# Two layers of cross-attention: layer 0's softmax weights transposed on VectorE in 32x32 blocks instead of on TensorE

## The chip, the cores and the metric

The kernel runs on one core of a Trainium2 chip. The metric is device time in microseconds: the median of several executions. A profiled execution has a time of its own, and a span, from its first instruction to its last, that is a little shorter.

The engines are named as the profile names them: PE is TensorE (matmuls), PEld its weight loads, DVE is VectorE, ACT is ScalarE, POOL is GpSimd, SP is the queue that issues most DMAs. L450 is line 450 of the kernel.

## The reference

All data are fp32. Eight batches have 100 query rows of width 1024 and a context of 1444 rows of width 512. Layer 0 is cross-attention with an output projection and a residual. Layer 1 takes its softmax over the query axis (axis 1, the 100 rows), adds its input and normalises.

```python
# x (8,100,1024), ctx_512 (8,1444,512)
# layer 0
Q = x @ Wq + bq; K = ctx @ Wk + bk; V = ctx @ Wv + bv
weights = softmax(Q @ K^T / sqrt(1024), axis=-1)        # (8,100,1444)
x = x + (weights @ V) @ Wo + bo
# layer 1
q = x @ Wq + bq; k = ctx @ Wk + bk; v = ctx @ Wv + bv
w = softmax(q @ k^T / sqrt(1024), axis=1)               # over the 100 rows
y = w @ v + x
out = (y - mean) * rsqrt(var + 1e-6) * gamma + beta
```

## The kernel before, in words

The kernel multiplies weight matrices with each other first (Wq with Wk, Wv with Wo), so that the long context never has to be projected: queries are brought into the 512-wide space of the context (`gT`), scores are taken against the raw context, and the weighted sum of raw context rows is projected afterwards. The big products are done with seven half-size products in place of eight.

**Layer 0's attention** is what the change touches. For each batch b there are three pieces of work.

- `scores0` (matmul L480, called "s" below): scores of the 100 queries against the context, 4 parts of the 512-wide axis times 11 pieces of the 1444 columns, so 44 matmuls. The context comes transposed (`cT`, four loads of 128x1444, `load_features`). The results fill four PSUM banks of the six that the pool `psum` has. VectorE moves them to the tile `p` (100x1444) with scale and bias (L492), takes the negative maximum (L494), ScalarE takes the exponential and the sum (L496), VectorE the reciprocal (L498) and the scaling (L499).
- `transposed` (L511, L512): `p` has queries on its rows, and the weighted sum needs context rows there. TensorE transposes 12 blocks of 100x120 (the last group 100x124), in three groups of four; each group goes into one PSUM bank, and ScalarE copies it to the tile `w`.
- `weighted_rows` (matmul L450, called "A"): 12 chunks of 120 context rows (the last one 124) times 4 parts of 128 columns, so 48 matmuls that add up in one PSUM bank of the pool `psum2`, which has two. VectorE copies the result to `A0T` (L463). The rows come through `load_rows` (L429, L433), four tiles of three chunks. Each load names 128 rows of every chunk, of which 120 are used.

**Order.** TensorE's order is the order of the program text; the other engines' orders are made by a scheduler from dependencies. The loop at L755 does iteration b: A of batch b, alternating one matmul for one with s of batch b+2, and the three transpose groups of batch b+1 put in after steps 28, 34 and 40. The scores of batches 0 and 1 and all of batch 0's transposes stand before the loop. In iterations 6 and 7 no scores are left, so A runs alone. After iteration 7 comes `project0`, then layer 1's queries and its own attention loop, which uses `weighted_rows` for its last two batches.

**Buffers.** Context tiles of both kinds share one pool of ten, and an iteration uses eight. SP issues a load when the tile of ten loads earlier is free. The `p` tiles come from a pool of three; the same three later hold three rows for layer 1 (`row_on_all`, L772, issued by POOL).

An fp32 matmul shows in the profile as two records, a transpose as one.

Of the kernel before, what the change touches and what calls it, by code (L numbers as in the profile page):

```python
# [24 lines left out]
F32 = mybir.dt.float32  # L25
# [14 lines left out]
GM = 4  # L40
NP, PM = 11, 3
CUTS = [S * n // NP for n in range(NP + 1)]
G = 4
GT = G * T
G1 = 5
# [5 lines left out]
def two_layer_cross_attention(ctx: ExitStack, tc: tile.TileContext, a: dict, out: bass.AP):  # L51
# [11 lines left out]
    def bank(name):  # L63
        return psum.tile([P, 512], F32, tag="ps", name=name)
# [11 lines left out]
    def row(name):  # L76
        return work.tile([P, E], F32, tag="row", name=name, bufs=3)

    def probabilities(name):
        return work.tile([P, S], F32, tag="prob", name=name, bufs=3)  # L80


    ones = const.tile([P, P], F32, tag="ones", name="ones")
# [9 lines left out]
    def column(name, layout):  # L93
        t = const.tile([P, EC], F32, tag=name, name=name)
        nc.gpsimd.dma_start(out=t, in_=a[name].rearrange(layout, c=EC))
        return t
# [3 lines left out]
        for n in ("L0_xattn_bq", "L0_xattn_bk", "L0_xattn_bv", "L1_xattn_bq", "L1_xattn_bk")  # L100
    }
    out_bias = column("L0_xattn_bo", "(c p) -> p c")

# [307 lines left out]
    def load_columns(b):  # L413

        src = a["ctxT"][b].rearrange("(c p) m -> p c m", p=P)
        for q in range(NQ):
            t = unit(f"cT_{b}_{q}")[:, : LC * (QR + MX)].rearrange("p (c m) -> p c m", c=LC)
            nc.sync.dma_start(out=t, in_=src[:, :, q * QR : (q + 1) * QR + MX])
            yield t

    def load_rows(b):

        src = a["ctx_512"][b]
        for q in range(NQ):
            t = unit(f"c_{b}_{q}").rearrange("p (c l) -> p c l", c=CQ)
            n = CQ - (q == NQ - 1)

            rows = bass.AP(src.tensor, src.offset + q * QR * L, [[L, P], [MR * L, n], [1, L]])
            nc.sync.dma_start(out=t[:, :n, :], in_=rows)  # L429
            if n < CQ:  # L430
                m = (MC - 1) * MR
                for r0, r1 in ((0, 112), (112, MR + MX)):
                    nc.sync.dma_start(out=t[r0:r1, n, :], in_=src[m + r0 : m + r1, :])  # L433
            yield t
# [6 lines left out]

        return MR + (MX if c == MC - 1 else 0)

    def weighted_rows(w, c, dst, name):

        ps = bank2(name)
        for m in range(MC):
            r = held(m)
            for k in range(LC):
                nc.tensor.matmul(  # L450
                    ps[:, k * T : (k + 1) * T],
                    c[m // CQ][:r, m % CQ, k * P : (k + 1) * P],
                    w[:r, m, :],
                    start=(m == 0 and k == 0),
                    stop=(m == MC - 1),
                    skip_group_check=True,
                )
                if (m, k) == (MC - 1, LC - 1):
                    src = ps[:, :GT].rearrange("p (c t) -> p c t", t=T)
                    if name.startswith("A1"):  # L460
                        nc.scalar.copy(dst, src)
                    else:
                        nc.vector.tensor_copy(dst, src)  # L463
                yield


    def scores0(s, cT):

        b = s["b"]
        p = probabilities(f"p_{b}")[:T]
        q0 = gT[0][b // G]
        t0 = b % G * T
        banks = [bank(f"s0_{b}_{n}") for n in range(0, NP, PM)]
        for k in range(LC):
            for n in range(NP):
                o = CUTS[n // PM * PM]
                nc.tensor.matmul(  # L480
                    banks[n // PM][:T, CUTS[n] - o : CUTS[n + 1] - o],
                    q0[:, k, t0 : t0 + T],
                    cT[k][:, CUTS[n] : CUTS[n + 1]],
                    start=(k == 0 and n % PM == 0),
                    stop=(k == LC - 1),
                    skip_group_check=True,
                )
                if (k, n) != (LC - 1, NP - 1):
                    yield
        for n, ps in zip(range(0, NP, PM), banks):  # L490
            o, e = CUTS[n], CUTS[min(n + PM, NP)]
            nc.vector.tensor_scalar(p[:, o:e], ps[:T, : e - o], SCALE, c0[:, b : b + 1], ALU.mult, ALU.add)  # L492
        negmax = small.tile([T, 1], F32, tag="negmax", name=f"negmax_{b}")
        nc.vector.tensor_reduce(negmax, p, AX.X, ALU.max, negate=True)  # L494
        total = small.tile([T, 1], F32, tag="total", name=f"total_{b}")
        nc.scalar.activation(p, p, AF.Exp, bias=negmax, accum_out=total)  # L496
        rtotal = small.tile([T, 1], F32, tag="rtotal", name=f"rtotal_{b}")
        nc.vector.reciprocal(rtotal, total)  # L498
        nc.vector.tensor_scalar(p, p, rtotal, None, ALU.mult)  # L499
        s["p"] = p  # L500
        yield

    def transposed(s):

        b, p = s["b"], s["p"]
        w = s["w"] = work.tile([P, MC, T], F32, tag="wT", name=f"w0_{b}", bufs=3)
        for m0 in range(0, MC, GM):
            ps = bank(f"pT_{b}_{m0}")
            r = shown(m0)
            for m in range(m0, m0 + GM):  # L510
                nc.tensor.transpose(ps[:r, (m - m0) * T : (m - m0 + 1) * T], p[:, m * MR : m * MR + r], ident[:T, :T])  # L511
            nc.scalar.copy(w[:r, m0 : m0 + GM, :], ps[:r, :GT].rearrange("p (c t) -> p c t", t=T))  # L512
            yield

    def add_to_queries(blocks, t0, width, banks):
        n = len(blocks) // len(banks)
# [42 lines left out]
    def scores1(s, cT, c1):  # L559

        b = s["b"]
        q1 = gT[1][b // G]
        t0 = b % G * T
        w = s["w"] = work.tile([P, MC, T], F32, tag="wT", name=f"w1_{b}", bufs=3)
        negmax = small.tile([P, MC], F32, tag="negmax1", name=f"negmax1_{b}")
        total = small.tile([P, MC], F32, tag="total1", name=f"total1_{b}")
        rtotal = small.tile([P, MC], F32, tag="rtotal1", name=f"rtotal1_{b}")  # L570
        for m0 in range(0, MC, GM):
            ps = bank(f"s1_{b}_{m0}")
            r = shown(m0)
            for m in range(m0, m0 + GM):
                o = m % CQ * MR
                for k in range(LC):
                    nc.tensor.matmul(  # L577
                        ps[:r, (m - m0) * T : (m - m0 + 1) * T],
                        cT[m // CQ][:, k, o : o + r],
                        q1[:, k, t0 : t0 + T],  # L580
                        start=(k == 0),
                        stop=(k == LC - 1),
                    )
                    if (m, k) != (m0 + GM - 1, LC - 1):
                        yield
            grp = slice(m0, m0 + GM)
            nc.vector.scalar_tensor_tensor(  # L587
                w[:r, grp, :],
                ps[:r, :GT].rearrange("p (c t) -> p c t", t=T),
                SCALE,  # L590
                c1[:r, t0 : t0 + T].unsqueeze(1).to_broadcast([r, GM, T]),
                ALU.mult,
                ALU.add,
            )
            nc.vector.tensor_reduce(negmax[:r, grp], w[:r, grp, :], AX.X, ALU.max, negate=True)  # L595
            for m in range(m0, m0 + GM):
                nc.scalar.activation(  # L597
                    w[:r, m, :], w[:r, m, :], AF.Exp, bias=negmax[:r, m : m + 1], accum_out=total[:r, m : m + 1]
                )
            nc.vector.reciprocal(rtotal[:r, grp], total[:r, grp])  # L600
            nc.vector.tensor_tensor(
                w[:r, grp, :], w[:r, grp, :], rtotal[:r, grp].unsqueeze(2).to_broadcast([r, GM, T]), ALU.mult
            )
            yield
# [146 lines left out]

    for b in range(2):
        run(scores0(batches[b], *loaded(load_features(b))))
    run(transposed(batches[0]))
    for b in range(B):  # L755
        nxt = b + 2 < B
        c, *cT = loaded(load_rows(b), *([load_features(b + 2)] if nxt else []))
        A = weighted_rows(batches[b]["w"], c, A0[b // G][:, :, b % G * T : (b % G + 1) * T], f"A0_{b}")
        s0 = scores0(batches[b + 2], *cT) if nxt else iter(())
        wT = transposed(batches[b + 1]) if b + 1 < B else iter(())  # L760
        for n in range(MC * LC):
            next(A)
            next(s0, None)
            if n in (28, 34, 40):
                next(wT, None)
        if b == 1:
            AS = value_sums(wvo)
    project0(AS, A0)

    def row_on_all(name):  # L770
        t = probabilities(name)[:, :E]
        nc.gpsimd.dma_start(out=t, in_=a[name].partition_broadcast(P))  # L772
        return t

    gT[1] = queries(1, wqk1, u1)
    c1 = [key_bias1(0)]
    bv1 = row_on_all("L1_xattn_bv")
    gamma = row_on_all("L1_xattn_gamma")
    beta = row_on_all("L1_xattn_beta")
    wv1 = weights.tile([P, LC, E], F32, tag="w", name="wv1")  # L780
    nc.gpsimd.dma_start(out=wv1, in_=a["L1_xattn_Wv"].rearrange("(c p) e -> p c e", p=P))
    for b in range(2):
# [7 lines left out]
    for b in range(B):  # L790
# [8 lines left out]
        if nxt:  # L799
            A = attend1(batches[b], c)  # L800
            s1 = scores1(batches[b + 2], *cT, c1[(b + 2) // G])
        else:
            A = weighted_rows(batches[b]["w"], c, A1[b][1], f"A1_{b}")
            s1 = iter(())
        for n in range(MC * LC):
            next(s1, None)
# [42 lines left out]
```

## Time and profile before

| | |
|---|---|
| median of 3 executions | 663.86 us (663.24 to 664.1) |
| the profiled execution | 663.64 us |
| its span | 661.7 us |
| TensorE busy | 650.8 us |
| VectorE busy | 359.8 us |
| ScalarE busy | 101.1 us |
| mean granted TensorE clock | 0.997 |
| layer 0: first score matmul to last A | 193.6 to 361.5 us |
| one iteration of the loop with scores | 20.7 us |
| its VectorE and ScalarE work | 5.65 and 3.07 us |

A busy time of TensorE counts instructions that overlap in its pipeline: what a matmul costs is read from the distance of two starts, not from the length that is listed for one. "Idle before" in a group's row is what its engine stood still ahead of it, and costs nothing where the engine isn't the one that sets the end.

### The profile page before, as it was taken

To read this page: it belongs to the slowest core of one execution; us is meant where nothing else is said; L and a number is where in the kernel's file an instruction comes from. 1 tells how busy PE (TensorE), PEld (TensorE's weight loads), DVE (VectorE), ACT (ScalarE), POOL (GpSimd) and SP (SyncE) were. 2 spreads that over 40 slices of the span, in tenths; PEclk is the share of its full clock that TensorE was granted. 3 is DMA by queue.
4 is the path that set the end of the run, shared out by engine and by line. 5 is a ranking of instruction groups with operands and counts; after the bars stand their busy time and mean duration, and the time that the engine had idled before them with its cause. 6 is when DMAs were issued, how large, how long until landed. Compare 5 with 4: busy or idle time off the path is not lost.

```text
span 661.7 us, 10338 instructions
## 1 busy us (share of the span) xinstructions
PE 650.8 (98%) x4360; PEld 552.8 (84%) x4360; DVE 359.8 (54%) x651; ACT 101.1 (15%) x295; POOL 22.8 (3%) x31
## 2 busy tenths in 40 slices
PE   9999999999999999999999999999999999999995
PEld 8885445568899999999999555579999999989992
DVE  5979638996055133312331875268443443566994
ACT  1010100321101111101120000204232322210000
POOL 2000000000000000000000000000000000001431
PEclk9999999999999999999999999999999999999998
DMA  9937046000099788988999003028888999820221
GB/s 295 378 121 264 0 121 255 1 0 1 26 347 310 247 291 291 315 291 293 311 327 345 30 0 127 1 87 285 267 297 297 307 307 296 299 78 1 77 74 50
DMA packets 60234, 127.51 MB, mean 193 GB/s; under 512 B 3928, under 2 KB 22872, under 8 KB 60188
## 3 DMA queue, kind: packets, MB, share of 16 engines
q1 hardware_dynamic: 57742, 119.82, 52.9%
q0 software_dynamic: 2048, 6.56, 3.1%
q8 instruction: 34, 0.56, 0.4%
q10 hardware_dynamic: 398, 0.47, 0.2%
q14 instruction: 12, 0.10, 0.0%
HBM read 123.56 MB, written 3.28 MB: 192 GB/s over the span
## 4 chain that ended last, share of the span: by engine, by line
PE 91%; DVE 5%; DMA 1%; issue 1%; SPq 1%; POOL 0%; POOLq 0%; DVEq 0%
PE A L450 14%; PE s L480 12%; PE s L577 12%; PE A L633 10%; PE qk_x L116 5%; PE g_x L116 5%; PE qk_y L116 4%; PE o_x L116 4%; PE g_y L116 3%; PE vo_x L116 3%; PE o_y L116 3%; PE qk_w L116 2%; PE vo_y L116 2%; PE g_w L116 2%; PE g_z L116 2%; PE o_w L116 1%
## 5 line engine op out<-in xcount | busy, mean ns | idle before, releaser
L450 PE MATMUL A<-w,c 120*128 120x100 f32 x960 | 146.2, 268 | 0.0
L450 PEld LDWEIGHTS A<-w,c 120*128 120x128 f32 x960 | 129.2, 191 | 0.1
L577 PE MATMUL s<-g1T,cT 128*120 128x100 f32 (+1 forms) x768 | 123.2, 261 | 0.0
L480 PE MATMUL s<-cT,g0T 128*100 128x131 f32 (+1 forms) x704 | 122.8, 275 | 0.0
L633 PE MATMUL A<-c,w 120*100 120x128 f32 (+1 forms) x576 | 110.7, 273 | 0.0
L577 PEld LDWEIGHTS s<-g1T,cT 128*120 128x120 f32 (+1 forms) x768 | 105.1, 185 | 0.6 <-issue 0.3
L480 PEld LDWEIGHTS s<-cT,g0T 128*100 128x100 f32 x704 | 87.8, 167 | 0.0
L633 PEld LDWEIGHTS A<-c,w 120*100 120x100 f32 (+1 forms) x576 | 74.0, 168 | 0.0
L492 DVE TENSOR_SCALAR p<-s,c 100x394 f32<-100x394 f32 (+2 forms) x32 | 18.8, 593 | 90.0 <-PE s L480 89.8
L597 ACT ACTIVATE w<-w,negmax 120x100 f32<-120x100 f32 (+1 forms) x96 | 35.1, 366 | 75.3 <-DVE negmax L595 75.3
L587 DVE SCALAR_TENSOR_TENSOR w<-s,c 120x400 f32<-120x400 f32 (+1 forms) x24 | 13.8, 574 | 41.6 <-PE s L577 41.6
L116 PE MATMUL qk_x<-qk 128*128 128x256 f32 x128 | 29.2, 387 | 0.0
L116 PEld LDWEIGHTS qk_x<-qk 128*128 128x128 f32 x128 | 24.5, 195 | 4.2 <-ACT qk L234 0.4
L512 ACT COPY w<-pT 120x400 f32<-120x400 f32 (+1 forms) x24 | 11.6, 493 | 100.3 <-PE pT L511 100.3
L708 POOL TENSOR_TENSOR rstd<-rstd,mhalf 100x1 f32<-100x1 f32 x8 | 11.8, 1477 | 230.6 <-DVE rstd L707 230.6
L600 DVE RECIPROCAL rtotal<-total 120x4 f32<-120x4 f32 (+1 forms) x24 | 4.2, 177 | 28.2 <-ACT w L597 28.2
L496 ACT ACTIVATE p<-p,negmax 100x1444 f32<-100x1444 f32 x8 | 12.0, 1499 | 46.9 <-DVE negmax L494 46.9
L519 DVE TENSOR_TENSOR xT<-xT,o_x 128x400 f32<-128x400 f32 (+1 forms) x24 | 13.7, 601 | 8.3 <-PE o_x L116 7.9
L597 ACT ACTIVATION_READ_ACCUMULATOR w<-w,negmax 120x1 f32 (+1 forms) x96 | 17.9, 187 | 0.0
L258 DVE SCALAR_TENSOR_TENSOR qk_L_xattn_bk<-qk,L_xattn_bk,qk_L_xattn_bk 128x1024 f32<-128x1024 f32 x14 | 17.8, 1271 | 0.0
L614 DVE TENSOR_REDUCE part<-w 120x100 f32<-120x1100 f32 x8 | 17.2, 2150 | 0.0
L323 DVE SCALAR_TENSOR_TENSOR kb<-xT,wqbk,kb 128x400 f32<-128x400 f32 x28 | 16.9, 626 | 0.2
(198 smaller groups left out, 862.2 us busy)
## 6 DMA issues: line engine op xcount, KB each, us to landing
c<-in_ctx SPq DMA_DIRECT2D x48, 768.0 KB, 8.1
cT<-in_ctxT SPq DMA_DIRECT2D x32, 728.0 KB, 6.4
cT<-in_ctxT SPq DMA_DIRECT2D x32, 722.0 KB, 5.9
c<-in_ctx SPq DMA_DIRECT2D x16, 512.0 KB, 7.6
vo<-in_L_xattn_Wo SPq DMA_DIRECT2D x8, 512.0 KB, 7.2
qk<-in_L_xattn_WqT SPq DMA_DIRECT2D x8, 512.0 KB
qk<-in_L_xattn_WqT SPq DMA_DIRECT2D x15, 256.0 KB, 5.4
qk<-in_L_xattn_WkT SPq DMA_DIRECT2D x15, 256.0 KB, 6.3
```

Of the source, the lines that this page charges most:

```text
L116: nc.tensor.matmul(banks[n // per][:, n % per * width : (n % per + 1) * width], lhs[i][:, n * P : (n + 1) * P], rhs[i], start=(fresh and i ...
L258: nc.vector.scalar_tensor_tensor(acc, src, cols[v][:, h : h + 1], acc, ALU.mult, ALU.add)
L323: nc.vector.scalar_tensor_tensor(acc, src, wqbk[:, k : k + 1], acc, ALU.mult, ALU.add)
L450: nc.tensor.matmul(ps[:, k * T : (k + 1) * T], c[m // CQ][:r, m % CQ, k * P : (k + 1) * P], w[:r, m, :], start=(m == 0 and k == 0), stop=( ...
L480: nc.tensor.matmul(banks[n // PM][:T, CUTS[n] - o : CUTS[n + 1] - o], q0[:, k, t0 : t0 + T], cT[k][:, CUTS[n] : CUTS[n + 1]], start=(k == ...
L492: nc.vector.tensor_scalar(p[:, o:e], ps[:T, : e - o], SCALE, c0[:, b : b + 1], ALU.mult, ALU.add)
L519: nc.vector.tensor_tensor(to, to, ps[:, : n * width].rearrange("p (n t) -> p n t", n=n), ALU.add)
L577: nc.tensor.matmul(ps[:r, (m - m0) * T : (m - m0 + 1) * T], cT[m // CQ][:, k, o : o + r], q1[:, k, t0 : t0 + T], start=(k == 0), stop=(k = ...
L587: nc.vector.scalar_tensor_tensor(w[:r, grp, :], ps[:r, :GT].rearrange("p (c t) -> p c t", t=T), SCALE, c1[:r, t0 : t0 + T].unsqueeze(1).to ...
L597: nc.scalar.activation(w[:r, m, :], w[:r, m, :], AF.Exp, bias=negmax[:r, m : m + 1], accum_out=total[:r, m : m + 1])
L614: nc.vector.tensor_reduce(part[:MR], w[:MR, :last, :].rearrange("p c t -> p t c"), AX.X, ALU.add)
L633: nc.tensor.matmul(ps[:T, part], w[:r, m, :], c[m // CQ][:r, m % CQ, part], start=(m == 0 and k == 0), stop=(m == MC - 1), skip_group_chec ...
```

## The change

1. `p` lies in three constant tiles of 1472 columns. POOL clears rows 96 to 127 and the columns from 1444 on of each once, at the start.
2. ScalarE moves the scores from PSUM with scale and bias; VectorE takes a maximum of each of the four parts and then of the four. ScalarE also does the scaling by the reciprocal.
3. Chunks of layer 0 have 128 context rows: eleven of 128 and one of 36. Their loads (`load_full_rows`) bring each row once.
4. The weights of a batch are transposed by VectorE: for each of four column quarters (of the 100 queries, padded to 128) and each of four row quarters of a chunk, one instruction transposes the 32x32 blocks of all 12 chunks (11 for the two row quarters that the last chunk doesn't have). That is 16 instructions a batch. A block's columns beyond 100 spill into the next chunk's place and are overwritten by a later instruction of the four quarters, which run from the last to the first.
5. For batches 0 and 7, TensorE still transposes the first four chunks in one group, with one ScalarE copy (`first_transposed`), and VectorE the other eight. The group stands directly ahead of the batch's A.
6. In the iteration b=5, two score matmuls stand beside each A, so that the last batch's scores end half-way through it.

```diff
+QD = 32
+SC = -(-S // P)
+SW = (SC - 1) * P + 2 * QD
+PT = 4
...
+    prob = [const.tile([P, SW], F32, tag=f"prob{n}", name=f"prob{n}") for n in range(3)]
+    for t in prob:
+        nc.gpsimd.memset(t[T // QD * QD :, :], 0.0)
+        nc.gpsimd.memset(t[:, S:], 0.0)
...
+    def load_full_rows(b):
...
+            full = S // P - q * CQ
+            n = min(CQ, full)
+            rows = src[q * CQ * P : (q * CQ + n) * P, :]
+            nc.sync.dma_start(out=t[:, :n, :], in_=rows.rearrange("(c p) l -> p c l", p=P))
+            if n < CQ:
+                nc.sync.dma_start(out=t[: S % P, n, :], in_=src[S // P * P :, :])
...
-        for n, ps in zip(range(0, NP, PM), banks):
-            o, e = CUTS[n], CUTS[min(n + PM, NP)]
-            nc.vector.tensor_scalar(p[:, o:e], ps[:T, : e - o], SCALE, c0[:, b : b + 1], ALU.mult, ALU.add)
+        parts = small.tile([T, len(banks)], F32, tag="maxima", name=f"maxima_{b}")
+        for n, ps in enumerate(banks):
+            o, e = CUTS[n * PM], CUTS[min((n + 1) * PM, NP)]
+            nc.scalar.activation(p[:, o:e], ps[:T, : e - o], AF.Identity, bias=c0[:, b : b + 1], scale=SCALE)
+            nc.vector.tensor_reduce(parts[:, n : n + 1], p[:, o:e], AX.X, ALU.max)
         negmax = small.tile([T, 1], F32, tag="negmax", name=f"negmax_{b}")
-        nc.vector.tensor_reduce(negmax, p, AX.X, ALU.max, negate=True)
+        nc.vector.tensor_reduce(negmax, parts, AX.X, ALU.max, negate=True)
...
-        nc.vector.tensor_scalar(p, p, rtotal, None, ALU.mult)
-        s["p"] = p
+        nc.scalar.activation(p, p, AF.Copy, scale=rtotal)
+        w = s["rows"] = weight_rows(f"w0_{b}")
+        s["w"] = w[:, : MC * T].rearrange("p (c t) -> p c t", t=T)
+        transposed(s, PT if b in (0, B - 1) else 0)
         yield
...
+    def transposed(s, m0):
...
+        for q in range(-(-T // QD) - 1, -1, -1):
+            for r in range(P // QD):
+                n = SC - m0 - (r * QD >= S % P)
+                nc.vector.transpose(
+                    blocks(w, r, m0 * T + q * QD, T, n),
+                    blocks(p, q, m0 * P + r * QD, P, n),
+                )
...
+    def blocks(t, quad, first, step, n):
...
+        rows = t[quad * QD : (quad + 1) * QD, first : first + QD]
+        return bass.AP(rows.tensor, rows.offset, [list(rows.ap[0]), [step, n], [1, QD]])
...
+    def first_transposed(s):
...
+        for m in range(PT):
+            nc.tensor.transpose(ps[:, m * T : (m + 1) * T], p[:, m * P : (m + 1) * P], ident[:T, :T])
+        nc.scalar.copy(s["rows"][:, : PT * T], ps[:, : PT * T])
...
-    run(transposed(batches[0]))
+    first_transposed(batches[0])
...
         for n in range(MC * LC):
             next(A)
-            next(s0, None)
-            if n in (28, 34, 40):
-                next(wT, None)
+
+            for _ in range(2 if b + 3 == B else 1):
+                next(s0, None)
+        if b == B - 2:
+            first_transposed(batches[B - 1])
```

More of the change, by code (lines that the diff above doesn't have):

```diff
@@ L77, in row, with weight_rows @@
         return work.tile([P, E], F32, tag="row", name=name, bufs=3)
-    def probabilities(name):
-        return work.tile([P, S], F32, tag="prob", name=name, bufs=3)
+    def weight_rows(name):
+        return work.tile([P, MC * T + QD * (-(-T // QD)) - T], F32, tag="wT", name=name, bufs=3)
     ones = const.tile([P, P], F32, tag="ones", name="ones")
@@ L419, in load_columns @@
             yield t
+    def load_full_rows(b):
+        src = a["ctx_512"][b]
+        for q in range(NQ):
+            t = unit(f"c_{b}_{q}").rearrange("p (c l) -> p c l", c=CQ)
+            full = S // P - q * CQ
[4 more added lines that the diff above has]
+                nc.sync.dma_start(out=t[: S % P, n, :], in_=src[S // P * P :, :])
+            yield t
     def load_rows(b):
@@ L442, in held, with held_full, weighted_rows @@
         return MR + (MX if c == MC - 1 else 0)
-    def weighted_rows(w, c, dst, name):
+    def held_full(c):
+        return min(P, S - c * P)
+    def weighted_rows(w, c, dst, name, held):
         ps = bank2(name)
@@ L472, in scores0 @@
         b = s["b"]
-        p = probabilities(f"p_{b}")[:T]
+        p = prob[b % len(prob)][:T, :S]
         q0 = gT[0][b // G]
@@ L498, in scores0 @@
         nc.vector.reciprocal(rtotal, total)
-        nc.vector.tensor_scalar(p, p, rtotal, None, ALU.mult)
-        s["p"] = p
+        nc.scalar.activation(p, p, AF.Copy, scale=rtotal)
+        w = s["rows"] = weight_rows(f"w0_{b}")
+        s["w"] = w[:, : MC * T].rearrange("p (c t) -> p c t", t=T)
+        transposed(s, PT if b in (0, B - 1) else 0)
         yield
[L503 to L513, printed above, removed]
+    def transposed(s, m0):
+        p, w = prob[s["b"] % len(prob)], s["rows"]
+        for q in range(-(-T // QD) - 1, -1, -1):
[9 more added lines that the diff above has]
+    def first_transposed(s):
+        b, p = s["b"], prob[s["b"] % len(prob)][:T]
+        ps = bank(f"pT_{b}")
+        for m in range(PT):
+            nc.tensor.transpose(ps[:, m * T : (m + 1) * T], p[:, m * P : (m + 1) * P], ident[:T, :T])
+        nc.scalar.copy(s["rows"][:, : PT * T], ps[:, : PT * T])
     def add_to_queries(blocks, t0, width, banks):
@@ L566, in scores1 @@
         t0 = b % G * T
-        w = s["w"] = work.tile([P, MC, T], F32, tag="wT", name=f"w1_{b}", bufs=3)
+        w = s["w"] = weight_rows(f"w1_{b}")[:, : MC * T].rearrange("p (c t) -> p c t", t=T)
         negmax = small.tile([P, MC], F32, tag="negmax1", name=f"negmax1_{b}")
@@ L753, in two_layer_cross_attention @@
         run(scores0(batches[b], *loaded(load_features(b))))
-    run(transposed(batches[0]))
+    first_transposed(batches[0])
     for b in range(B):
         nxt = b + 2 < B
-        c, *cT = loaded(load_rows(b), *([load_features(b + 2)] if nxt else []))
-        A = weighted_rows(batches[b]["w"], c, A0[b // G][:, :, b % G * T : (b % G + 1) * T], f"A0_{b}")
+        c, *cT = loaded(load_full_rows(b), *([load_features(b + 2)] if nxt else []))
+        A = weighted_rows(batches[b]["w"], c, A0[b // G][:, :, b % G * T : (b % G + 1) * T], f"A0_{b}", held_full)
         s0 = scores0(batches[b + 2], *cT) if nxt else iter(())
-        wT = transposed(batches[b + 1]) if b + 1 < B else iter(())
         for n in range(MC * LC):
             next(A)
-            next(s0, None)
-            if n in (28, 34, 40):
-                next(wT, None)
+            for _ in range(2 if b + 3 == B else 1):
+                next(s0, None)
+        if b == B - 2:
+            first_transposed(batches[B - 1])
         if b == 1:
@@ L768, in two_layer_cross_attention, with row_on_all @@
     project0(AS, A0)
-    def row_on_all(name):
-        t = probabilities(name)[:, :E]
+    def row_on_all(name, n):
+        t = prob[n][:, :E]
         nc.gpsimd.dma_start(out=t, in_=a[name].partition_broadcast(P))
@@ L776, in two_layer_cross_attention @@
     c1 = [key_bias1(0)]
-    bv1 = row_on_all("L1_xattn_bv")
-    gamma = row_on_all("L1_xattn_gamma")
-    beta = row_on_all("L1_xattn_beta")
+    bv1 = row_on_all("L1_xattn_bv", 0)
+    gamma = row_on_all("L1_xattn_gamma", 1)
+    beta = row_on_all("L1_xattn_beta", 2)
     wv1 = weights.tile([P, LC, E], F32, tag="w", name="wv1")
@@ L802, in two_layer_cross_attention @@
         else:
-            A = weighted_rows(batches[b]["w"], c, A1[b][1], f"A1_{b}")
+            A = weighted_rows(batches[b]["w"], c, A1[b][1], f"A1_{b}", held)
             s1 = iter(())
```

## The prediction

> **What bounds the kernel now.** I read the page first: who is busy, and when.
>
> ```profile
> span 661.7 us, 10338 instructions
> PE 650.8 (98%) x4360; PEld 552.8 (84%) x4360; DVE 359.8 (54%) x651; ACT 101.1 (15%) x295; POOL 22.8 (3%) x31
> PE   9999999999999999999999999999999999999995
> PEclk9999999999999999999999999999999999999998
> ```
>
> TensorE works in every slice at the full clock; nothing else comes near. The change touches layer 0's attention loop (193.6 to 361.5 us). The chain of waits, asked for 185 to 370 us, holds TensorE alone there:
>
> ```profile
> by line: PE A L450 43.3%; PE s L480 43.0%; PE pT L511 4.5%; PE qk_y L116 3.5%; PE o_x L116 1.8%; PE o_y L116 1.5%; PE o_z L116 1.5%; PE c_ps L392 0.5%; PE wqbk L299 0.5%; PE u L299 0.2%
> ```
>
> So a TensorE instruction taken out here shortens the end by what it occupies, if nothing else becomes late. The listed durations (268 ns for A) overlap; prices are start to start. A piece of the timeline, TensorE rows (start, length, engine, line):
>
> ```profile
> 270.76 0.36 PE L450 MATMUL A<-w,c 120*128 120x100 f32 x2
> 270.96 0.39 PE L480 MATMUL s<-cT,g0T 128*100 128x131 f32 x2
> 271.18 0.51 PE L511 MATMUL pT<-ident,p 100*120 100x100 f32 x4
> 271.53 0.39 PE L450 MATMUL A<-w,c 120*128 120x100 f32 x2
> ...
> 271.98 0.36 PE L450 MATMUL A<-w,c 120*128 120x100 f32 x2
> ...
> 272.40 0.36 PE L450 MATMUL A<-w,c 120*128 120x100 f32 x2
> ```
>
> A matmul is two records, a transpose one. One A and one s repeat every 0.427 us (271.98 to 272.40; later 272.40 to 273.68 for three). Four transposes push the next A back by 0.35 us (271.18 to 271.53), and that first step lasts 0.45 instead of 0.427: **0.37 us a group of four**. A iterations repeat every 20.735 us (first evictions L492 at 230.70, 251.45, 272.18), and 44 x 0.427 + 4 x 0.22 + 3 x 0.37 = 20.8 accounts for it.
>
> Last, the busy time by stretch (PE, PEld, DVE, ACT, POOL; then clock, DMA share, GB/s), one iteration and the stretch where loads run ahead:
>
> ```profile
> 255.20:275.90 20.70, 20.70 (x198) 20.70 (x198) 5.65 (x8) 3.07 (x5) 0.00 (x0) 1.00 0.85 285
> 349.50:361.50 12.00, 12.00 (x109) 12.00 (x108) 0.57 (x1) 0.21 (x1) 0.51 (x1) 1.00 1.02 349
> ```
>
> VectorE has 15 of 20.7 us free. The loads move 285 GB/s where 349 is reached.
>
> [...] No StreamTranspose is in this trace. [...] LDWEIGHTS takes 191 ns for 120x128, 192 for 124x128, 190 for 128x128.
>
> **The change, part by part.** The nearest rows of before:
>
> ```profile
> L595 DVE TENSOR_REDUCE negmax<-w 120x4 f32<-120x400 f32 x16 | 9.0, 565 | 0.4
> L496 ACT ACTIVATE p<-p,negmax 100x1444 f32<-100x1444 f32 x8 | 12.0, 1499 | 46.9 <-DVE negmax L494 46.9
> L345 ACT ACTIVATE g1T<-g_x,u 128x400 f32<-128x400 f32 x6 | 3.6, 593 | 64.1 <-PE g_x L116 58.8 <-DVE g1T L350 5.1
> L512 ACT COPY w<-pT 120x400 f32<-120x400 f32 x16 | 7.8, 492 | 84.5 <-PE pT L511 84.5
> ```
>
> 1. *Transposes off TensorE.* Batches 1 to 6 lose 3 groups each: 18 x 0.37 = **-6.7 us**, all on the path. Batches 0 and 7 keep one group of 12 blocks' three, but now nothing stands between it and the A that needs its copy. Group 0.35, about 0.25 until the copy starts (213.2 to 213.8 in before, group included), copy 0.49: 1.1 us. Before, batch 0's 12 transposes took 1.03, batch 7's three groups 1.03 inside A_6. So each of the two is **+0.05 to +0.2** (the upper end if batch 1's last eviction, about 0.5 us on ScalarE, holds the copy): +0.2 together.
> 2. *Scores at double pace for b=5.* The chain in order of time has 88 s alone in 19.85 us, 0.2256 each, and A alone as 66 records in 7.35 us, 0.2229 each; a pair takes 0.427. The iteration becomes 22 x (0.427 + 0.226) + 26 x 0.223 = 20.15 instead of 44 x 0.427 + 4 x 0.22 = 19.65: **+0.5 us**.
> 3. *Chunks of 128.* Still 12 chunks, 48 matmuls a batch; only the rows change (128 x 11 + 36 for 120 x 11 + 124): 0 on TensorE, since 190 to 192 ns show no slope with the rows; bound 0.5 us either way (768 records, 0.65 ns each). Loads fall from 1532 to 1444 rows, 3.14 to 2.96 MB a batch, and SP issues 8 DMAs fewer. The 36-row piece is small beside its lead of some 20 us (ten buffers for eight loads an iteration; landing takes 6 to 8 us).
> 4. *VectorE's transposes.* 16 instructions a batch, 8 of 12 blocks of 32 and 8 of 11[...].
> 5. *Evictions to ScalarE, maxima in parts, normalising on ScalarE.* ScalarE gains 4 x 0.6 + 1.5 and loses 3 x 0.49: 3.1 becomes 5.5 us an iteration of 19.6. VectorE loses 4 x 0.6 + 1.66 + 0.97 and gains 4 x 0.5 + 0.2 + 8.65: 5.65 becomes 11.5. Both are hidden if the chain below is on time; 0.
> 6. *Start.* Six memsets on POOL behind its six small DMAs, the last of which it issues at 4.6 us; its next work in before is layer 1's bias row at 316 us (L772). Those three rows now wait for VectorE's transposes of batches 5 to 7, not TensorE's, and are used only in layer 1. VectorE's sums of the first weight product run beside the memsets, with TensorE busy on products that need none of them: 0, bound +0.3.
>
> **Who waits for whom.** A_b's first matmul now waits for VectorE; behind it on TensorE stands everything. For batches 2 to 6, from the start of an iteration b: the last scores came 0.9 us before, ScalarE's last eviction ends at -0.4, its maximum at 0.1, then VectorE must evict A_b (0.7), negmax 0.9, exp 2.7, reciprocal 2.9, ScalarE's scaling 4.5, transposes 13.2. Needed at 19.65: 6.4 us spare. Batch 1 is tightest, since its maxima queue behind batch 0's transposes: scaling of batch 0 done at 208.2 (L499 started at 207.65 before; 1.0 off for the shorter maximum, 1.5 on for ScalarE's scaling), transposes to 214.7, batch 1's chain 5.7 (maxima 2.0, negmax 0.2, exp 1.75, reciprocal 0.2, scaling 1.5) to 220.4, transposes to 229.1, needed at 214.4 + 19.65 = 234.0: 4.9 spare. Batch 0's own blocks from chunk 4 on are needed at step 16, 221.2. Batch 7 ends its scores 14.35 into b=5, is scaled at 19.0, and its group is due at 30.85. A_5's eviction stands behind batch 7's transposes on VectorE, but its bank is wanted only by A_7, 5 us later.
>
> **Sum.** -6.7 + 0.2 + 0.5 = -6.0 us. The profiled execution took 663.64 (span 661.7, 1.94 around it); the median is 663.86, 0.2 above. So 657.6 to 657.9; I say **657.7**. After the loop all shifts together: TensorE stays the bound to the end.
>
> **Rivals.**
> - *Transposes at two cycles an element (slower).* For: no row here prices a 4-byte transpose. [...] batch 1 is ready at 218.7 + 5.7 + 14.8 = 239.2, a stall of 5.2; each of batches 2 to 6 then takes 5.7 + 14.8 = 20.5 against 19.65, 0.85 x 5 = 4.2 more. -6.0 + 9.4 = +3.4: about **667**. It decides from about 0.89 us an instruction; below 0.73 there is no stall at all.
> - *Loads become the bound.* An iteration of 19.65 us needs 5.91 MB, 301 GB/s. For: share 0.85 now, and b=5 wants batch 7's features by step 16. Against: 349 GB/s is shown, and SP's queue stood 72.4 us in 22 waits for s and 30.1 us in 8 for A between 175 and 370 us: it waits for free buffers. Were 290 the ceiling, the iteration would be 20.4: 6 x 0.75 = 4.5 of the 6.0 lost, about **662**.
> - *The reached gain is only part.* The two bare groups wait longer than 1.1 us, or each A_b pays a VectorE hand-over of 0.1 to 0.3: 1 to 3 us less, about **660**.
> - *It doesn't do what it says: A_0 and A_7 wait for VectorE from the first chunk on.* Then the kept groups buy nothing. Against: in the changed order A_0's first matmul waits for its load and ScalarE alone, step 16 for VectorE. Price: 214.7 in place of 214.4, so **658**.
>
> **How the numbers follow.** Forecast (gain of 5 to 7) 0.68; part gain or loads, 1.4 to 5 us, 0.15; a stall that eats the gain, 0.04; slower by the transposes 0.13. A change under 0.2% (1.3 us) can't be told from none here. Hence faster 0.83, same 0.04, slower 0.13. Range 656.2 (items 1 and 2 a little better) to 662.0 (part gain); the slower case is left out.
>
> **What would show it.** Right: PE's L511 rows gone but for 8 transposes, iterations about 19.6 us apart, StreamTranspose at 0.52 to 0.56 us, TensorE's idle before A under 1 us in each of two places. Wrong: A_1 waiting on VectorE's w for microseconds, transposes near 0.9 us, or A and s waiting on DMA.

## The result, and the profile after

The changed kernel takes 660.64 us (median of 4, 659.84 to 661.43) against 663.79: a ratio of 0.9953, 95% interval 0.9936 to 0.9971. It is 3.15 us faster where 6.1 were forecast. The page of its profiled execution (659.84 us):

```profile
span 658.1 us, 10293 instructions
PE 645.4 (98%) x4272; PEld 545.2 (83%) x4272; DVE 404.5 (61%) x771; ACT 120.1 (18%) x313; POOL 27.3 (4%) x37
PE   9999999999999999999999999999999999999994
PEclk9999999999999999999999999999999999999998
```

TensorE is still busy in every slice, and the 88 transposes are gone (4360 records, now 4272). VectorE has 45 us more. The chain of waits for 185 to 370 us, the answer to the line shown of before:

```profile
by line: PE A L476 44.6%; PE s L506 42.8%; PE o_x L125 4.1%; PE qk_y L125 3.3%; PE o_z L125 1.5%; PE o_y L125 1.5%; ACT prob L519 0.5%; ACT w L558 0.5%; PE wqbk L308 0.5%; PE c_ps L401 0.5%; PE pT L557 0.3%; PE u L308 0.2%; issue 0.1%
```

The transposes' 4.5% are down to 0.3% and 1% of ScalarE has come, but A has a larger share than before, 44.6%, though its matmuls are as many. What the weight loads of the loop waited for (us in total, times, longest):

```profile
PEld A L476 <- ACT w L558: 1.6, 2, 0.8
```

So no A waits for VectorE or for a load; only the two bare groups show, 0.8 us each. The busy time of one iteration (PE, PEld, DVE, ACT, POOL; clock, DMA share, GB/s) and VectorE's own groups (busy, mean ns, idle before):

```profile
253.50:273.40 19.90, 19.90 (x186) 19.65 (x186) 11.75 (x24) 5.34 (x7) 0.00 (x0) 1.00 0.85 301
L542 DVE STREAM_TRANSPOSE w<-prob 32x384 f32<-32x384 f32 x48 | 27.3, 568 | 10.4 <-ACT prob L527 9.4
L542 DVE STREAM_TRANSPOSE w<-prob 32x352 f32<-32x352 f32 x48 | 25.8, 538 | 1.1
```

The iteration is 19.91 us (A's evictions at 253.93 and 273.85) where 19.6 to 19.65 were expected. It went from 20.735, so 0.83 was gained of 1.11. The place of the missing 0.28 is in TensorE's timeline, at the end of an iteration, where four A stand alone. First before, then after (start, length, what):

```profile
275.52 0.39 PE L480 MATMUL s<-cT,g0T 128*100 128x132 f32 x2
275.75 1.25 PE L450 MATMUL A<-w,c 124*128 124x100 f32 x10
276.84 0.39 PE L480 MATMUL s<-cT,g0T 128*100 128x131 f32 x2
```

```profile
272.36 0.39 PE L506 MATMUL s<-cT,g0T 128*100 128x132 f32 x2
272.68 1.53 PE L476 MATMUL A<-w,c 36*128 36x100 f32 x10
274.04 0.39 PE L506 MATMUL s<-cT,g0T 128*100 128x131 f32 x2
```

From s to s it was 1.32 us and is 1.68: the first A of 36 rows starts 0.32 after the s before it, not 0.23, and the ten records (eight of 36 rows, two of the next batch's 128) take 1.36, not 1.09. No wait is listed for it. The rest of the iteration gives 0.08 of these 0.36 us back: its 44 pairs of A and s take 0.424 us each, where they took 0.426.

The weight loads (PEld) show what is different there. First a chunk of 128 rows and its weights, then the 36-row chunk's weights, after the change:

```profile
272.05 0.30 PEld L476 LDWEIGHTS A<-w,c 128*128 128x128 f32 x2
272.16 0.36 PE L476 MATMUL A<-w,c 128*128 128x100 f32 x2
272.68 1.36 PEld L476 LDWEIGHTS A<-w,c 36*128 36x128 f32 x10
```

The weights of a full chunk begin to load 0.11 us ahead of their matmul, beside the matmul before. Those of the first 36-row matmul begin together with it, at 272.68, so this load is not hidden.

The loop as a whole, from its first score matmul to the first `o_x`, before and then after:

```profile
193.40 1.86 PE L480 MATMUL s<-cT,g0T 128*100 128x131 f32 x15
361.31 2.88 PE L116 MATMUL o_x<-A0T,vo 128*128 128x400 f32 x8
```

```profile
193.00 2.20 PE L506 MATMUL s<-cT,g0T 128*100 128x131 f32 x18
357.27 2.95 PE L125 MATMUL o_x<-A0T,vo 128*128 128x400 f32 x8
```

It takes 167.9 and 164.3 us: 3.6 us less, where the prediction's sum has 6.0. That the loop starts 0.4 us earlier is put down to scatter and not to the change: in the kernels of the experiments below the first score comes at 192.98 to 193.71. After the loop everything keeps the same distance (3.96 us at 616). The two profiled executions differ by 3.8 us and the medians by 3.15: the four executions of the changed kernel spread over 1.6 us, and the profiled one is the shortest of them.

### The profile page after: what moved, and what is told of

Read it like the earlier page. It is cut to its first block, busy times and chain, and to the rows that moved or that the text cites. A ratio compares the mean times of both kernels' runs of the same rounds, so it can differ in the third digit from the quotient of the medians.

```text
span 658.1 us, 10293 instructions
## 1 busy us (share of the span) xinstructions
PE 645.4 (98%) x4272; PEld 545.2 (83%) x4272; DVE 404.5 (61%) x771; ACT 120.1 (18%) x313; POOL 27.3 (4%) x37
## 4 chain that ended last, share of the span: by engine, by line
PE 93%; DVE 4%; DMA 1%; issue 1%; POOL 0%; SPq 0%; ACT 0%; POOLq 0%; DVEq 0%
PE A L476 14%; PE s L506 12%; PE s L622 12%; PE A L678 10%; PE qk_x L125 6%; PE g_x L125 5%; PE qk_y L125 4%; PE o_x L125 4%; PE g_y L125 3%; PE vo_x L125 3%; PE o_y L125 3%; PE qk_w L125 2%; PE qk_z L125 2%; PE vo_y L125 2%; PE g_z L125 2%; PE g_w L125 2%
## 5 line engine op out<-in xcount | busy, mean ns | idle before, releaser
L476 PE MATMUL A<-w,c 128*128 128x100 f32 (+1 forms) x960 | 143.9, 269 | 1.2 <-ACT w L558 1.2
L476 PEld LDWEIGHTS A<-w,c 128*128 128x128 f32 (+1 forms) x960 | 127.9, 190 | 3.3 <-ACT w L558 1.6
L506 PE MATMUL s<-cT,g0T 128*100 128x131 f32 (+1 forms) x704 | 119.3, 276 | 0.0
L542 DVE STREAM_TRANSPOSE w<-prob 32x352 f32<-32x352 f32 (+3 forms) x128 | 66.5, 519 | 15.3 <-ACT prob L527 12.5
L519 ACT ACTIVATE prob<-s,c 100x394 f32<-100x394 f32 (+2 forms) x32 | 17.8, 562 | 98.7 <-PE s L506 98.4
L520 DVE TENSOR_REDUCE maxima<-prob 100x1 f32<-100x394 f32 (+2 forms) x32 | 16.4, 528 | 24.3 <-ACT prob L519 24.0
```

The costliest lines, as they stand in the source:

```text
L476: nc.tensor.matmul(ps[:, k * T : (k + 1) * T], c[m // CQ][:r, m % CQ, k * P : (k + 1) * P], w[:r, m, :], start=(m == 0 and k == 0), stop=( ...
L506: nc.tensor.matmul(banks[n // PM][:T, CUTS[n] - o : CUTS[n + 1] - o], q0[:, k, t0 : t0 + T], cT[k][:, CUTS[n] : CUTS[n + 1]], start=(k == ...
L519: nc.scalar.activation(p[:, o:e], ps[:T, : e - o], AF.Identity, bias=c0[:, b : b + 1], scale=SCALE)
L520: nc.vector.tensor_reduce(parts[:, n : n + 1], p[:, o:e], AX.X, ALU.max)
L542: nc.vector.transpose(blocks(w, r, m0 * T + q * QD, T, n), blocks(p, q, m0 * P + r * QD, P, n),)
```

## The experiments

Theory A: the 36-row chunk costs TensorE about 0.37 us a batch that a chunk of more rows doesn't. Theory B: the loss comes with the transposes on VectorE, or with their waits. A kernel's ratio is against the kernel before, timed beside it (663.7 to 663.9).

### Chunks of 120 rows again

```diff
-SC = -(-S // P)
+SC, QP = 12, 120
+QL = S - (SC - 1) * QP
...
-        return min(P, S - c * P)
+        return QP if c < SC - 1 else QL
...
-                    blocks(p, q, m0 * P + r * QD, P, n),
+                    blocks(p, q, m0 * QP + r * QD, QP, n),
```

The loads take the rows from multiples of 120 on, again 128 rows for every chunk but the last, as before the change.

> The changed kernel with layer 0's chunks back at 120 rows (the last 124), transposed by VectorE all the same; all 16 transposes then have 12 blocks. Theory A (the 36-row chunk costs TensorE about 0.37 us a batch): the last 4 A of an iteration take about 1.1 instead of 1.46 us, the iteration 19.6 instead of 19.91, and the kernel about 3 us less than the changed one, near 657.5. Theory B (the lost 2.5 us have another cause, say VectorE's transposes slowing TensorE's reads): iteration stays at 19.9, time at 660.6.

Measured: 658.49 us (658.38 to 658.57), ratio 0.9922 (0.9907 to 0.9936). A's evictions and the end of an iteration:

```profile
254.19 0.57 DVE L491 COPY A0T<-A 128x400 f32<-128x400 f32 x1
273.82 0.57 DVE L491 COPY A0T<-A 128x400 f32<-128x400 f32 x1
```

```profile
272.75 1.25 PE L478 MATMUL A<-w,c 124*128 124x100 f32 x10
```

The iteration is 19.63 us, and the listed length of the ten records is 1.25 as before the change (1.53 in the changed kernel). VectorE transposes as much as in the changed kernel and more (96 instructions of 570 ns in the six full batches, for 48 of 568 and 48 of 538). Theory B falls. The loads are different too in this run; the next one leaves them as the change has them.

### The 36-row chunk between full ones

```diff
-        for m in range(MC):
+        order = [*range(10), 11, 10] if name.startswith("A0") else range(MC)
+        for m in order:
```

> The changed kernel with the 36-row chunk taken before the last full one, so that in iterations 0 to 4 its four A alternate with scores of 128 rows. If the cost belongs to each change between 36 and 128 rows (about 0.18 us each, 2 a batch before, 8 now), an iteration gets 6 x 0.18 = 1.1 us longer (21.0) and the kernel about 5.4 us slower than the changed one, near 666. If it belongs to the 36-row matmuls themselves, the iteration stays at 19.9 and the time at 660.6.

Measured: 665.91 us (665.56 to 666.23), ratio 1.0033 (1.0020 to 1.0046); the iteration is 21.01 us. TensorE's timeline:

```profile
273.27 0.36 PE L477 MATMUL A<-w,c 128*128 128x100 f32 x2
273.47 0.39 PE L507 MATMUL s<-cT,g0T 128*100 128x131 f32 x2
273.79 0.46 PE L477 MATMUL A<-w,c 36*128 36x100 f32 x2
274.18 0.47 PE L507 MATMUL s<-cT,g0T 128*100 128x132 f32 x2
274.58 0.46 PE L477 MATMUL A<-w,c 36*128 36x100 f32 x2
```

A pair of 128 rows takes 0.424 us, a pair with a 36-row A 0.79 (273.79 to 274.58): 0.18 for each of the two changes. The matmuls and the loads are the same as in the changed kernel, only with eight changes of height an iteration for two: six more, and 1.10 us more. So the cost is of the change from one height to the other, not of the short matmul. Among themselves the 36-row matmuls keep the pace of full ones: in the changed kernel seven of their records start from 272.87 to 273.54, 0.112 us apart, and two records of a full A take 0.223.

What TensorE does at such a change isn't shown; the runs give its price.

### Where the height starts to matter

```diff
-SC, QP = 12, 120
+SC, QP = 12, 125      # 69 rows in the last chunk
...
+SC, QP = 12, 126      # 58 rows
```

> Chunks of 125 rows, the last one 69. If what counts is that the last chunk has fewer rows than the others, the loss stays (iteration 19.9)[...].

> Chunks of 126 rows, the last one 58. With a limit between 69 and 58 rows[...] the loss is here as in the changed kernel: iteration 19.9, near 660.6. With a loss proportional to the missing rows it is about three quarters of it: 19.8.

Measured: 657.88 us (657.36 to 658.21), ratio 0.9912 (0.9897 to 0.9927) with 69 rows, and 660.96 (660.77 to 661.14), ratio 0.9959 (0.9945 to 0.9973) with 58. A's evictions, for 125 and then for 126, give iterations of 19.63 and 19.99 us:

```profile
254.24 0.57 DVE L491 COPY A0T<-A 128x400 f32<-128x400 f32 x1
273.86 0.57 DVE L491 COPY A0T<-A 128x400 f32<-128x400 f32 x1
```

```profile
254.69 0.57 DVE L491 COPY A0T<-A 128x400 f32<-128x400 f32 x1
274.68 0.57 DVE L491 COPY A0T<-A 128x400 f32<-128x400 f32 x1
```

The last chunk's row of the timeline, in the same order:

```profile
272.79 1.25 PE L478 MATMUL A<-w,c 69*128 69x100 f32 x10
```

```profile
273.51 1.53 PE L478 MATMUL A<-w,c 58*128 58x100 f32 x10
```

58 rows cost as much as 36 (iterations of 19.99 and 19.91 us), 69 cost nothing (19.63, as with 120 and 124). The loss doesn't grow with the missing rows. Its limit lies between 58 and 69; no height between them was run.

### The kernel before, with the changed one's chunks

```diff
-        c, *cT = loaded(load_rows(b), *([load_features(b + 2)] if nxt else []))
+        c, *cT = loaded(load_full_rows(b), *([load_features(b + 2)] if nxt else []))
...
-                nc.tensor.transpose(ps[:r, (m - m0) * T : (m - m0 + 1) * T], p[:, m * MR : m * MR + r], ident[:T, :T])
+                nc.tensor.transpose(ps[:r, (m - m0) * T : (m - m0 + 1) * T], p[:, m * P : m * P + r], ident[:T, :T])
```

> The kernel before (TensorE transposes, VectorE evictions) with the chunks and loads of the changed one: eleven of 128 rows and one of 36, with one more ScalarE copy a batch. If the 36-row chunk costs 0.37 us a batch by itself, and 44 pairs of 128 rows gain 0.1 us, an iteration takes 21.0 instead of 20.74 us and the kernel about 2.3 us more, near 666. If the chunk only hurts beside VectorE's transposes, it stays at 663.7.

Measured: 666.58 us (665.65 to 666.68), ratio 1.0036 (1.0023 to 1.0050); iterations of 21.03 us. Without VectorE's transposes the chunk costs about the same: the kernel is slower by 2.7 us, and its loop, from first score to first `o_x`, by 2.4.

### One score matmul beside each A to the end

```diff
-            for _ in range(2 if b + 3 == B else 1):
-                next(s0, None)
+            next(s0, None)
```

This is on top of the 125-row chunks.

> Chunks of 125 and 69 rows, and one score matmul beside each A in iteration b=5 too, as before. If the double pace costs 0.5 us because pairs are cheaper than A and s alone, this gains it: near 657.4. If the double pace is needed to have batch 7's weights in time, A_7 waits for VectorE at its fifth chunk and the kernel is slower than with double pace.

Measured: 657.89 us (657.46 to 658.93), ratio 0.9911 (0.9896 to 0.9926): the medians show no difference to 657.88. The trace shows what was meant: iteration b=5 takes 19.62 us (evictions at 312.89 and 332.51), against about 20.1 with double pace, and the only wait of A is again 0.8 us for ScalarE twice. Batch 7's weights are in time without the double pace. Its 0.5 us is there in the traces, where the loop takes 161.4 us instead of 161.9, and in the spans, 655.5 to 655.8 us against 655.6 to 656.4. Only the time outside the span hides it: 1.8 to 3.3 us in this kernel's four executions, 1.7 to 1.8 in the other's.

### The two TensorE groups put in earlier

```diff
-    for b in range(2):
-        run(scores0(batches[b], *loaded(load_features(b))))
-    first_transposed(batches[0])
+    run(scores0(batches[0], *loaded(load_features(0))))
+    for n, _ in enumerate(scores0(batches[1], *loaded(load_features(1)))):
+        if n == NP * LC - 6:
+            first_transposed(batches[0])
...
-        if b == B - 2:
-            first_transposed(batches[B - 1])
+            if b == B - 2 and n == 40:
+                first_transposed(batches[B - 1])
```

> The same, and the two TensorE groups of batches 0 and 7 put in earlier: batch 0's five scores before the end of batch 1's, batch 7's after step 40 of iteration b=6, so that their copies run beside other matmuls. Each bare group stood TensorE about 0.75 us; both gone give 1.5 us: near 656. If ScalarE's queue (batch 1's evictions) holds the copy, less.

Measured: 655.91 us (655.30 to 656.23), ratio 0.9876 (0.9860 to 0.9893), the shortest time of all: 7.9 us less than the kernel before. TensorE around batch 0's group:

```profile
212.23 0.51 PE L559 MATMUL pT<-ident,prob 100*128 100x100 f32 x4
212.58 1.29 PE L508 MATMUL s<-cT,g0T 128*100 128x131 f32 x10
213.71 0.36 PE L478 MATMUL A<-w,c 125*128 125x100 f32 x2
```

The scores go on 0.35 us after the group and A starts when they end; no wait of TensorE is listed in the loop any more. The gain over the kernel of the section before is 2.0 us in the medians for the 1.5 expected, and 1.7 in the loop of the profiled executions.

### Every VectorE transpose twice

```diff
+                for _ in range(2):
                     nc.vector.transpose(
```

> The changed kernel with every VectorE transpose done twice (18.4 us a full batch instead of 9.2). By the chain of the prediction A_1 then waits some 11 us for VectorE and each of A_2 to A_6 about 4: some 30 us more, near 690, with TensorE's waits for the transposes' tile. If there was more cover than reckoned, less; if the transposes were not on any chain at all, 660.6.

Measured, one execution: 700.9 us. The waits of A's weight loads:

```profile
PEld A L476 <- DVE w L543: 14.9, 3, 11.2
PEld A L476 <- issue: 10.9, 4, 2.9
```

The profile names VectorE's tile `w` for three of the waits and nothing ("issue") for four. A_1 stands 11.2 us, as reckoned, and the iterations come every 24.27 us; the prediction's chain with this price, 5.7 + 18.4, is 24.1. So the chain through ScalarE and VectorE is the right one, and the changed kernel is on the near side of it. The total is 10 us above the expectation. Some 7 of them lie in A_7, which it left out: from A_7's first matmul to the first `o_x` it takes 18.3 us (380.05 to 398.34), for 11.1 in the changed kernel, and 2.5 of these are a wait for VectorE at the fifth chunk. TensorE's granted clock was lower in this execution, 0.967 in the mean of the span (0.996 in the changed kernel's) and 0.92 from 248.2 to 272.5 us; how much of A_7's time that is wasn't separated. Why it was lower stays open; there is one execution.

### Evictions and scaling on VectorE again

```diff
-            nc.scalar.activation(p[:, o:e], ps[:T, : e - o], AF.Identity, bias=c0[:, b : b + 1], scale=SCALE)
+            nc.vector.tensor_scalar(p[:, o:e], ps[:T, : e - o], SCALE, c0[:, b : b + 1], ALU.mult, ALU.add)
...
-        nc.scalar.activation(p, p, AF.Copy, scale=rtotal)
+        nc.vector.tensor_scalar(p, p, rtotal, None, ALU.mult)
```

> The changed kernel with the scores moved from PSUM, and the weights scaled, by VectorE again (four maxima kept). VectorE then has some 14.9 us of work in an iteration of 19.9, and batch 1's chain ends about as before. If both are hidden, as the prediction held, nothing changes: iteration 19.91, near 660.6. If ScalarE's part was needed to keep VectorE in time, A_1 waits for the transposes' tile and the kernel is slower by what shows there.

Measured: 661.81 us (median of 20, 660.55 to 663.51), ratio 0.9974 (0.9966 to 0.9982). The iteration is 19.91 as expected, with 16.0 us of VectorE's work in it instead of 14.9, and A never waits for the transposes, but one new wait is there:

```profile
PEld s L506 <- DVE prob L519: 0.7, 1, 0.7
```

It is a score of batch 2 at 216.15: its bank still holds batch 1's scores, whose evictions stand behind batch 0's transposes on VectorE until 215.47. So ScalarE's evictions are worth something at one place, 0.7 us. The loop of the profiled execution is longer by just that (164.95 us for 164.27). The other half microsecond between 661.81 and 660.64 isn't in this trace. The granted clock differs among the 20 executions: the nine with less than 0.995 all took over 662.6 us, and the median of the other eleven is 661.06; the changed kernel's four all had 0.996 or more.

## Why the prediction was right or wrong, point by point

**TensorE is the bound and transposes off it shorten the end: right.** With the height of the chunks put back, an iteration takes 19.63 us, 1.105 less than before; three groups at 0.37 are 1.11. With chunks of 125 and 69 rows the loop takes 161.9 us (193.71 to 355.65), 6.0 less than before, which is the prediction's sum, and the kernels take 657.88 and 658.49 us, against 657.7 forecast.

**The bare groups: right.** From group to A 1.15 us each (212.85 to 214.00, 345.06 to 346.21), 1.1 to 1.2 forecast. The run with the two groups put in earlier shows that the placement takes their waits out again.

**The double pace: right in size** (0.5 us in the trace), and needless.

**The chunks of 128: this step failed.** Item 3 of the sum put them at 0 on TensorE with a bound of 0.5 us, because weight loads of 120, 124 and 128 rows take the same time (191, 192 and 190 ns in the trace of before). That a chunk of 36 rows costs no more either was not shown: the fewest rows of a weight load in that trace are 100. In the changed kernel a weight load of 36 rows takes 187 ns, and a record of a 36-row A 0.112 us among its like, as one of a full A, but neither answers the question: the eleven chunks that grew were considered, the one that shrank to 36 was not, and what costs is going over from one height to the other, about 0.18 us each way.

In the traces the term is about 0.35 us in each of the eight batches. In a paired iteration it is 0.36 (19.99 against 19.63, for 58 and 69 rows). In the three without a paired score at the end it is 0.34 to 0.40 between the same two runs, if what follows the last chunk, the transposes or the first `o_x`, is counted in. That is 2.8 us; the full chunks give back 0.08 in each of the first five iterations (19.91 for 19.99), 0.4 in all. The 2.4 that are left are the distance between the loop's gain, 3.6 us, and the 6.0 of the sum. In the medians it is 660.64 - 657.88 = 2.8 us, with their scatter.

**VectorE's transposes: right.** 568 and 538 ns an instruction; sixteen take 9.18 us for 8.65, an estimate of the author's that no row of before shows. The rival of slower transposes is out: both forms are below the 0.73 us under which it saw no stall, and 568 - 434 ns for 128 more elements (the 32x256 form takes 434) is 1.05 ns an element. The chain, whose times rest on that estimate, came out as drawn: batch 2's transposes end 13.3 us into the iteration b=1 (at 247.28, forecast 13.2), batch 1's at 229.9 with 4.1 us to spare (forecast 229.1 and 4.9).

**Evictions to ScalarE at no cost: right**, and the last run adds that they keep one wait of 0.7 us away.

**Loads: right.** The iteration shown moves 301 GB/s, as the prediction worked out and more than the 290 that the rival took for a ceiling, and no matmul of the loop waits for a load.

**The rival that A_0 and A_7 wait for VectorE from the first chunk on** is out: the only waits there are the 0.8 us each for ScalarE's copy.

**The rival of a partial gain** gave about this time, 660, but for another reason: it thought of longer bare groups or a hand-over from VectorE at each A, and neither is there. The stated range reaches as far as the measured time only because of this rival, so that it holds the time is luck.

## What to carry to other kernels

When a tiling is changed to use all 128 rows, look at the remainder: a last piece of 58 or 36 rows among full ones cost TensorE two changes of height each time, 0.36 us together, while rows spread evenly (120 and 124), or a remainder of 69, cost nothing (iterations of 19.63 us both). A price read for an instruction alone says nothing of its neighbours; ask what happens between two that differ. A transposed block that is copied before use belongs some matmuls ahead of its use, not right before it: right before it a weight load of TensorE waited 0.8 us for the copy, with the group put in earlier none did.

## What the runs showed of the hardware

- Going from matmuls of 128 rows to such of 36 and back costs about 0.18 us each way at a granted clock of 1.00, with no wait listed: 0.79 us for a pair instead of 0.424. With 58 rows the two ways cost 0.36 together; between 128 or 125 rows and 69 nothing is seen. The 36-row matmuls among themselves run at the pace of full ones (0.112 us a record).
- StreamTranspose of fp32 takes 1.05 ns an element of a lane plus 0.17 us an instruction, worked out from two forms (434 ns for 256, 568 for 384 elements).
- A pair of A and s takes 0.424 us with 128 rows in A and 0.426 with 120 to 126 (worked out from iterations of 19.91, 19.63 and 19.99 us); why stays open.
